# Two selective-scan layers on one Trainium2 core: sums of two groups take turns in the halves of one PSUM bank, their copies to y stand in four steps, and the short unit and the output stage share work differently

## The chip, the cores and the metric

The kernel runs on one core of a Trainium2 chip. A core has TensorE (PE; its weight loads are listed apart as PEld), VectorE (DVE), ScalarE (ACT) and GpSimd (POOL), which read and write 128 partitions of on-chip memory: SBUF, and PSUM, where PE leaves its results. SyncE (SP) issues the DMAs. The metric is the device time of one launch in microseconds; the median of three runs is given.

## The reference

The input x has 8 images of 64 x 64 positions with 96 channels. Two layers follow each other, each `x = x + conv_ref(groupnorm(x))`. Cut to what matters:

```python
# layer 0; layer 1 has the same frame
xp, z = split(x @ in_proj_w.T)                 # 192 channels each
xc = silu(depthwise_conv3x3(xp) + conv_b)
xs = cross_scan(xc)                            # 4 directions: by rows, by columns, both reversed
dts, Bs, Cs = split(x_proj(xs), [6, 16, 16])
delta = softplus(dt_projs(dts) + dt_bias)      # one per channel and position
def step(h, (u_t, d_t, B_t, C_t)):             # 16 states per channel, 4096 positions
    h = exp(d_t * A) * h + d_t * B_t * u_t
    return h, sum_states(h * C_t)
y = cross_merge(scan(step)) + u * D
out = (layernorm(y) * silu(z)) @ out_proj_w.T

# layer 1, in place of the recurrence
decay = exp(cumsum(dt * A))
h = decay * cumsum(dt * B * u / (decay + 1e-12))
y = sum_states(h * C) + u * D
```

In layer 1 `decay` falls to nothing after the first positions of a direction, and there h is nothing too. The kernel computes the first 160 positions of each direction at most, and fewer for the higher states.

## The kernel before

**Tiling.** Every image is done by itself. Its 4096 positions are cut into four pieces of T = 1024; the 192 channels into two halves of 96 and those into three groups of 32. One *set* is 32 channels x 4 states on the 128 partitions by 1024 positions. Four sets cover the 16 states of a group, twelve a *job* (a half of the channels in one piece of one direction), so an image has 32 jobs and 384 sets. One launch goes through a beginning and then, for each image, a layer-0 scan and an output stage. Layer 1 of the image before is not a stage by itself: its convolution and the preparation of its inputs lie beside the scan, its scan is a *short unit* of 6 sets (960 wide) at the end of the next image's sets, and its output stage is done together with that of the next image. The last image's layer 1 stands alone at the end, in `scan_last`.

**The scan's order.** `scan_rows` writes the order out by hand under `tc.manual_schedule()`, one set per step n. `at(i)` is set n + i. In one step every engine works at another set:

- SP: `fetch` and `replicate` (the broadcast loads of `dt_rep`, `dtu_rep`, `b_rep`, `c_rep`), four to five steps ahead.
- DVE: `advance_set(at(0))`: the product `set = drive * b` (L970; in three of four sets), then the scan itself (L983), in place in `set`.
- ACT: `keep_state` (L994, the last column), `fill(at(1))`: `decay = exp(rate * dt)` into one of two PSUM buffers (L936), `drive(at(2))`: a copy of `dtu` into a PSUM tile (L953) once in a group, `release(at(-4))`: four copies of 32 x 256 from the group's sums `acc` into y (L1065; the tile is named `map` in the profile) once in a group.
- POOL: `read_out(at(-1))`: `out = set * c` (L999), and `early(at(2))`: the product `dtu * b` of every fourth set (L960).
- PE: `collect(at(-3))`: for a group's first set four matmuls that put the skip term or the old y into the sums (L1026), and for each set four matmuls that add up the four states (`w_gather`, L1035). The sums stand in `acc`, one PSUM bank in a pool of one buffer.

After `collect` come the step's planned stages: `ps_dt` (L690) and the transposes `ps_sp` (L724) on PE, with ACT's steps on `arena` between them (L701, L702, L736 and others), which make dt and dt * u of the job after next; the projection `ps_proj` (L570); and the convolution of layer 1 (L1102, `ps_conv`, nine taps for each piece). Once in four steps (`late`, the step in which a new group's first set is collected) the planned stages stand ahead of `collect`.

A short set goes the same way with other parts: DVE makes the product (L970), one fused product with the gate (L973: `(cum + 1) * set`) and two scans (L978); ACT makes the gate, four tanh in place in `cum` (L947), the decay (L932) and a `drive` copy; PE has 16 matmuls per set (L1012, which is shown for two sets), and ACT scales the sums into `y_short` (L1055).

**The output stage.** `out_phase` goes through chunks of 512 positions, eight per layer and image. A table `order` gives each operation a lag in chunks, and every step issues each operation for another chunk: load; `first_sum` (POOL); `mean` (PE, L1529) and `centre` (DVE, L1606); `square` (ACT, L1572) and `second_sum` (POOL, L1599, in place in `sq`); `variance` (PE, L1550, one chunk into 32 rows of `ps_var`); `roots` (ACT) and a Newton step (DVE, L1522 to L1524) for four chunks at once, which leave 1/sqrt(var) in 32-row strips of `r`; `gates` (PE, the z part of the in-projection, L1543) and `silu` (ACT, L1589); `row` (PE, L1534: a matmul over all 128 rows of `r` with a picking matrix, which spreads one chunk's strip to 96 rows); `scale` (DVE, L1610); `affine` (ACT, L1577, twice, one for each half of the channels); `product` (POOL); `project` (PE, L1562, `ps_out`); `end` and `store`.

PSUM has eight banks of 128 x 512. The scan uses four for `decay`, two for `drive`, one for `acc` and one (`pmisc`) for all planned stages; the output stage two for `mean`, two for `ps_var`, two for z, one for `ps_r` and one for `ps_out`.

## Time and profile before

| what | value |
|---|---|
| median of three runs | 12128.35 us (12126.23 to 12153.42) |
| the profiled execution | 12140.8 us, span 12138.9 us, mean granted PE clock 0.765 |
| products with c on POOL (L999) | 3120 of 2364 ns, 7308.8 us |
| scans with a state on DVE (L983) | 2304 of 2344 ns, 5361.8 us |
| scans without a state on DVE (L983) | 768 of 2286 ns, 1743.0 us |
| decay on ACT (L936) | 3072 of 1115 ns, 3424.4 us |
| products with b on DVE (L970) | 2352 of 1198 ns, 2818.4 us |
| sums over states on PE (L1035) | 24576 of 518 ns, 2394.3 us |
| convolution on PE (L1102) | 4032 of 689 ns, 2201.6 us |
| copies of sums to y on ACT (L1065) | 3072 of 479 ns, 1471.7 us |

All of it is one execution on the chip, taken by the hardware profiler. An engine's busy time counts neither waits nor the issue of DMAs. PE's matmuls overlap in the pipeline, so that count times mean is more than the busy time, and the distance between the starts of two groups says what they cost PE. "L999" is line 999 of the kernel before; in the changed kernel the same operations stand a few lines lower. In the groups, "out<-in" are the program's names of tiles, followed by partitions x elements; after the second bar stand the idle time of the engine just before these instructions and what ended most of it. In the timeline a row gives the start, the length, the engine, the line, the operation with its tiles, and in brackets how long it waited and for what; x4 means that four such instructions are drawn together. In the windows a row begins with the stretch and its length and ends with the granted PE clock, the busy share of the DMA engines and GB/s.

By the trace's times the beginning ends at 127 us; the eight scans, each without its short unit, take 1275 to 1307 us; between two scans lie 99 us (after the first image) or 185 to 190 us with the short unit and the output stage of two layers. The end after the last scan takes from 11723 to 12139 us.

### The profile page before, as it was taken

The page shows a single profiled execution, that of the slowest core. Times are in us where ns is not written, and L with a number is a line of the kernel's source. Part 1 is how long each engine was busy: PE and PEld are TensorE (multiplying, and loading weights), DVE is VectorE, ACT ScalarE, POOL GpSimd, SP SyncE. Part 2 cuts the span into 40 slices and gives each one's busy share as a digit, 9 for nine tenths or more (in the row PEclk, how much of TensorE's full clock was granted, in tenths as well). Part 3 has the DMA queues.
Part 4 walks back from the last instruction along what each step waited for, and adds up shares of the span by engine and source line. Part 5 has one row for each costly group of instructions (what it writes and reads, how often), then busy time and mean ns, then how long its engine had stood idle before and what let it go on. Part 6 is the DMA issues. An engine that isn't in the chain of part 4 may idle for free. (4 is left out here: it accounts for less than half of the span.)

```text
span 12138.9 us, 147546 instructions
## 1 busy us (share of the span) xinstructions
PE 8813.3 (73%) x50950; PEld 4023.1 (33%) x50950; DVE 10895.6 (90%) x6783; ACT 9090.1 (75%) x14944; POOL 10525.2 (87%) x4751
## 2 busy tenths in 40 slices
PE   6765577777877777777777767877687776876567
PEld 2332233332333323333333323333333332333222
DVE  8999799997999979999799997999879998899985
ACT  6777677777777777777777777777777777777775
POOL 6999799996999969999699986999879997799983
PEclk7776677778777787777877788777787777877677
DMA  4444444444444444444444454444544445444441
GB/s 133 149 165 156 137 149 165 164 164 144 164 154 159 157 145 167 162 165 153 152 148 166 164 160 147 166 163 155 165 138 164 161 165 164 135 157 157 155 145 57
DMA packets 670708, 1862.43 MB, mean 153 GB/s; under 512 B 186728, under 2 KB 201486, under 8 KB 669949
## 3 DMA queue, kind: packets, MB, share of 16 engines
q1 hardware_dynamic: 662781, 1840.30, 45.8%
q10 hardware_dynamic: 7168, 12.59, 0.3%
q8 instruction: 405, 6.64, 0.2%
q14 instruction: 354, 2.90, 0.1%
HBM read 1539.34 MB, written 313.28 MB: 153 GB/s over the span
## 5 line engine op out<-in xcount | busy, mean ns | idle before, releaser
L999 POOL TENSOR_TENSOR out<-set,c_rep 128x1024 f32<-128x1024 f32 x3120 | 7308.8, 2364 | 820.1 <-PE acc L1035 350.2
L983 DVE TENSOR_TENSOR_SCAN set<-decay,state,set 128x1024 f32<-128x1024 f32 x2304 | 5361.8, 2344 | 360.0 <-ACT decay L936 118.6
L936 ACT ACTIVATE decay<-dt_rep,w_a 128x1024 f32<-128x1024 f32 x3072 | 3424.4, 1115 | 429.1 <-DVE set L983 427.2
L970 DVE TENSOR_TENSOR set<-drive,b_rep 128x1024 f32<-128x1024 f32 x2352 | 2818.4, 1198 | 35.2 <-DMA b_rep<-x_dblr 17.6
L1035 PE MATMUL acc<-out,w_gather 128*32 128x256 f32 x24576 | 2394.3, 518 | 8.5 <-POOL out L999 8.1
L1102 PE MATMUL ps_conv<-edged,taps 96*96 96x512 f32 (+1 forms) x4032 | 2201.6, 689 | 9.8 <-ACT arena L702 8.1
L960 POOL TENSOR_TENSOR set<-dtu_rep,b_rep 128x1024 f32<-128x1024 f32 x768 | 1856.8, 2418 | 96.9 <-DMA b_rep<-x_dblr 31.0
L983 DVE TENSOR_TENSOR_SCAN set<-decay,set 128x1024 f32<-128x1024 f32 x768 | 1743.0, 2286 | 147.7 <-ACT decay L936 53.1
L724 PE MATMUL ps_sp<-w_eye,arena 128*96 128x128 f32 x7680 | 1167.3, 317 | 707.0 <-ACT arena L736 672.9
L1026 PE MATMUL acc<-map,w_eye 96*32 96x256 f32 x4608 | 577.5, 584 | 1352.3 <-ACT map L1065 1085.4
L1065 ACT COPY map<-acc 32x256 f32<-32x256 f32 x3072 | 1471.7, 479 | 66.3 <-PE acc L1035 25.8
L724 PEld LDWEIGHTS ps_sp<-w_eye,arena 128*96 128x96 f32 x7680 | 1011.1, 148 | 1012.6 <-ACT arena L736 788.6
L1035 PEld LDWEIGHTS acc<-out,w_gather 128*32 128x32 f32 x24576 | 880.9, 140 | 1390.2 <-issue 1066.3
L994 ACT COPY state<-set 128x1 f32<-128x1 f32 x2304 | 433.1, 188 | 1061.2 <-DVE set L983 1053.3
L690 PE MATMUL ps_dt<-w_dtw,x_dbl 7*128 7x96 f32 x3840 | 803.1, 371 | 533.2 <-ACT arena L736 426.9
L1102 PEld LDWEIGHTS ps_conv<-edged,taps 96*96 96x96 f32 (+1 forms) x4032 | 701.9, 189 | 1275.5 <-issue 1188.6
L690 PEld LDWEIGHTS ps_dt<-w_dtw,x_dbl 7*128 7x128 f32 x3840 | 700.0, 269 | 778.5 <-ACT arena L736 499.9
L953 ACT COPY drive<-dtu_rep 128x1024 f32<-128x1024 f32 (+1 forms) x816 | 816.5, 1001 | 40.1 <-DMA dtu_rep<-dtu_far 19.2
L701 ACT ACTIVATE arena<-ps_dt 128x384 f32<-128x384 f32 x480 | 235.9, 492 | 647.1 <-PE ps_dt L690 631.0
L1026 PEld LDWEIGHTS acc<-map,w_eye 96*32 96x32 f32 x4608 | 104.0, 125 | 1676.3 <-ACT map L1065 1299.5
L600 POOL TENSOR_TENSOR arena<-arena,map 96x1024 f32<-96x1024 f32 x240 | 635.5, 2648 | 12.9 <-ACT arena L736 11.7
L570 PE MATMUL ps_proj<-map,w_wx 96*78 96x512 f32 x512 | 402.7, 923 | 9.9 <-ACT map L305 6.1
(204 smaller groups left out, 7718.6 us busy)
## 6 DMA issues: line engine op xcount, KB each, us to landing
dt_rep<-dt_far SPq DMA_DIRECT2D x768, 512.0 KB
dtu_rep<-dtu_far SPq DMA_DIRECT2D x768, 512.0 KB
b_rep<-x_dblr SPq DMA_DIRECT2D x256, 512.0 KB
c_rep<-x_dblr SPq DMA_DIRECT2D x256, 512.0 KB
b_rep<-x_dblc SPq DMA_DIRECT2D x256, 512.0 KB
c_rep<-x_dblc SPq DMA_DIRECT2D x256, 512.0 KB
dt_far<-arena SPq DMA_DIRECT2D x240, 384.0 KB
dtu_far<-arena SPq DMA_DIRECT2D x240, 384.0 KB
```

What stands on the lines that cost most here:

```text
L690: nc.tensor.matmul(job["ps"][:, j, :], unit["x_dbl"][: R + 1, at : at + P], w["dtw0"][:, k, h * C : (h + 1) * C], start=True, stop=True,)
L724: nc.tensor.matmul(job["ps"][:C, j * P : (j + 1) * P], job[name][:, s * BLOCKS + j, :], w["whole_eye"], is_transpose=True, start=i == 0, s ...
L936: nc.scalar.activation(s["decay"], s["group"]["dt"], AF.Exp, scale=rate)
L953: nc.scalar.copy(s["group"]["drive"], s["group"]["dtu"])
L960: nc.gpsimd.tensor_tensor(s["buf"], s["group"]["dtu"], b, ALU.mult)
L970: nc.vector.tensor_tensor(s["buf"], s["group"]["drive"], b, ALU.mult)
L983: nc.vector.tensor_tensor_scan(ordered(s["buf"], unit), ordered(s["decay"], unit), ordered(s["buf"], unit), 0.0 if unit["nth"] == 0 else s ...
L999: nc.gpsimd.tensor_tensor(s["out"], s["buf"], s["unit"]["c", s["i"]], ALU.mult)
L1026: nc.tensor.matmul(acc, lhs[:, GC * g : GC * (g + 1)], positions(old[:, h, :], unit["column"], unit["t0"] + at, n), start=True, stop=False ...
L1035: nc.tensor.matmul(acc, w["gather"], s["out"][:, at : at + n], start=False, stop=s["i"] == NS - 1, skip_group_check=True,)
L1065: nc.scalar.copy(yk, like(acc, unit["column"]))
L1102: nc.tensor.matmul(job["ps"][:C, :], taps[l][:k, h, tap, :], edged[:k, tap // 3 : tap // 3 + rows, tap % 3 : tap % 3 + WW], start=tap == 0 ...
```

## The change

There are three parts.

**The sums.** The bank `acc` is one tile for the whole scan, and its two halves of 256 columns are handed out in turn to the groups. `release` copies one of the four strips per step, at steps 4 to 7 after the group's last set; for the image's last whole group all four come at once. The `late` order is gone: `collect` always stands ahead of the planned stages. In `scan_last` two banks take turns, as the pool's two buffers did before.

**The short unit.** The product with b of a short set is made by POOL one step ahead, `gate` writes to a PSUM tile of the `drive` pool, and the copy `drive` is left out for short sets. The copies to `y_short` (now `release_short`) do not change.

**The output stage.** `row` is issued for two chunks at once, and each matmul reads only its 32-row strip of `r` and of the picking matrix; `ps_r` has two banks and `ps_var` one. `variance` is issued for four chunks at once; the sums of squares wait for it in `squares`, a tile with four buffers. The second half of `affine` goes from ACT to DVE. A chunk is loaded one step later, and `x_in` has six buffers.

```diff
@@ scan_rows
+                bank = pacc.tile([P, MM], F32, name="acc0")
+                accs = cycle([bank[:, : T // Q], bank[:, T // Q :]])
...
+                    last = n - 4 == whole - 1
...
-                    drive(at(2), False, pdrive)
-                    drive(at(1), True, pdrive)
-                    release(at(-4), y, beside)
-                    gate(at(1))
+                    drive(at(2), pdrive)
+                    release_short(at(-4), beside)
+                    for a in range(Q):
+                        release(at(-4 if last else -4 - a), a, y)
+                    gate(at(1), pdrive)
+                    early(at(1), True, work)
                     read_out(at(-1), work)
-                    early(at(2), work)
-                    late = (n + 1) % NS == 0
-                    if not late:
-                        collect(at(-3), xc, y, pacc)
+                    early(at(2), False, work)
+                    collect(at(-3), xc, y, accs)
                     for stage in plan.pop(n, []):
                         stage()
-                    if late:
-                        collect(at(-3), xc, y, pacc)
@@ by_gpsimd
-        return s["i"] == NS - 1
+        return s["i"] == NS - 1 or s["unit"]["short"]
@@ gate
+            s["gate"] = pdrive.tile([P, T], F32, name="drive")[:, :HT]
...
-                nc.scalar.activation(cum, cum, AF.Tanh, bias=half_log, scale=rate)
+                cum, out = blocks(s["group"]["cum"], i), blocks(s["gate"], i)
+                nc.scalar.activation(out, cum, AF.Tanh, bias=half_log, scale=rate)
@@ collect
-            group["acc"] = pacc.tile([P, MM], F32, name="acc0")
+            group["acc"] = next(accs)
@@ release(s, a, y): one strip a of a group
+        if not s or s["unit"]["short"] or s["i"] < NS - 1 or a in s.setdefault("gone", []):
             return
+        s["gone"].append(a)
-        for a in range(Q):
...
+        nc.scalar.copy(yk, like(acc, unit["column"]))
@@ out_phase
-            tc.tile_pool(name="pvar", bufs=2, space=PSUM) as pvar,
+            tc.tile_pool(name="pvar", bufs=1, space=PSUM) as pvar,
-            tc.tile_pool(name="prow", bufs=1, space=PSUM) as prow,
+            tc.tile_pool(name="prow", bufs=2, space=PSUM) as prow,
@@ row(c): nothing for odd c, else both chunks of the pair
+                for c in (c, c + 1):
+                    q = c % Q
+                    rows = slice(GC * q, GC * (q + 1))
...
+                        w["pick"][rows, q, :],
+                        groups[c // Q]["r"][rows, :],
@@ variance(c): nothing before the fourth chunk, then all four
+                for q in range(Q):
+                    nc.tensor.matmul(
+                        group["var"][GC * q : GC * (q + 1), :],
+                        w["avg"][:, :GC],
+                        held[c - Q + 1 + q].pop("squares"),
@@ affine
-                for h in range(NH):
...
+                nc.scalar.activation(
+                    first, first, AF.Identity, bias=shift[:, 0:1], scale=gain[:, 0:1]
+                )
+                nc.vector.tensor_scalar(
+                    second, second, gain[:, 1:2], shift[:, 1:2], ALU.mult, ALU.add
+                )
@@ second_sum
-                nc.gpsimd.tensor_tensor(sq[:, 0, :], sq[:, 0, :], sq[:, 1, :], ALU.add)
+                held[c]["squares"] = brief.tile([C, MM], F32, name="squares", bufs=Q)
+                nc.gpsimd.tensor_tensor(
+                    held[c]["squares"], sq[:, 0, :], sq[:, 1, :], ALU.add
+                )
@@ order
-                (load, 5), (mean, 1), (row, 8), (gates, 7), (variance, 3), (project, 10),
+                (load, 6), (mean, 1), (row, 8), (gates, 7), (variance, 3), (project, 10),
@@ loaded
-            x = xpool.tile([C, MM], F32, name="x_in", bufs=7)
+            x = xpool.tile([C, MM], F32, name="x_in", bufs=6)
```

More of the change, by code (lines that the diff above doesn't have):

```diff
@@ L2 @@
 from contextlib import ExitStack, contextmanager
+from itertools import cycle
 import concourse.bass as bass
@@ L446, in scan_rows @@
             total = len(sets)
+            whole = sum(not s["unit"]["short"] for s in sets)
             plan = plan(pmisc)
@@ L936, in fill, with gate, drive, early @@
         nc.scalar.activation(s["decay"], s["group"]["dt"], AF.Exp, scale=rate)
-    def gate(s):
+    def gate(s, pdrive):
         if s and s["unit"]["short"]:
+            s["gate"] = pdrive.tile([P, T], F32, name="drive")[:, :HT]
             for i in range(NS):
                 rate = w["a1_half"][:, column(s) + i :][:, :1]
-                cum = blocks(s["group"]["cum"], i)
-                nc.scalar.activation(cum, cum, AF.Tanh, bias=half_log, scale=rate)
-    def drive(s, short, pdrive):
-        if s and s["i"] == 0 and s["unit"]["short"] == short:
+                cum, out = blocks(s["group"]["cum"], i), blocks(s["gate"], i)
+                nc.scalar.activation(out, cum, AF.Tanh, bias=half_log, scale=rate)
+    def drive(s, pdrive):
+        if s and s["i"] == 0 and not s["unit"]["short"]:
             s["group"]["drive"] = pdrive.tile([P, T], F32, name="drive")[:, : s["unit"]["n"]]
             nc.scalar.copy(s["group"]["drive"], s["group"]["dtu"])
-    def early(s, work):
-        if s and by_gpsimd(s):
+    def early(s, short, work):
+        if s and by_gpsimd(s) and s["unit"]["short"] == short:
             s["buf"] = work.tile([P, T], F32, name="set", bufs=SETS)[:, : s["unit"]["n"]]
@@ L973, in advance_set @@
             nc.vector.scalar_tensor_tensor(
-                buf, s["group"]["cum"], 1.0, buf, ALU.add, ALU.mult
+                buf, s["gate"], 1.0, buf, ALU.add, ALU.mult
             )
@@ L999, in read_out, with collect @@
             nc.gpsimd.tensor_tensor(s["out"], s["buf"], s["unit"]["c", s["i"]], ALU.mult)
-    def collect(s, xc, y, pacc):
+    def collect(s, xc, y, accs):
         if not s:
@@ L1042, in collect, with release_short, release @@
             )
-    def release(s, y, beside):
-        if not s or s["i"] < NS - 1 and not s["unit"]["short"]:
+    def release_short(s, beside):
+        if not s or not s["unit"]["short"]:
             return
         unit, h, g = s["unit"], s["group"]["h"], s["group"]["g"]
-        if unit["short"]:
-            if h == g == 0:
-                ys_far[unit["b"]] = dram.tile([NH, P, NG * HEAD], F32, name="ys_far", bufs=2)
-            if g == 0:
-                unit["y"] = beside.tile([P, MM], F32, tag="conv_out", name="y_short")
-            part = unit["y"][:, g * HEAD : (g + 1) * HEAD]
-            nc.scalar.mul(part, s["group"]["acc"][:, :HEAD], 0.5)
-            if g == NG - 1:
-                nc.sync.dma_start(ys_far[unit["b"]][h], unit["y"][:, : NG * HEAD])
+        if h == g == 0:
+            ys_far[unit["b"]] = dram.tile([NH, P, NG * HEAD], F32, name="ys_far", bufs=2)
+        if g == 0:
+            unit["y"] = beside.tile([P, MM], F32, tag="conv_out", name="y_short")
+        part = unit["y"][:, g * HEAD : (g + 1) * HEAD]
+        nc.scalar.mul(part, s["group"]["acc"][:, :HEAD], 0.5)
+        if g == NG - 1:
+            nc.sync.dma_start(ys_far[unit["b"]][h], unit["y"][:, : NG * HEAD])
+    def release(s, a, y):
+        if not s or s["unit"]["short"] or s["i"] < NS - 1 or a in s.setdefault("gone", []):
             return
+        s["gone"].append(a)
+        unit, h, g = s["unit"], s["group"]["h"], s["group"]["g"]
         n = T // Q
-        for a in range(Q):
-            yk = positions(
-                y[GC * g : GC * (g + 1), h, :], unit["column"], unit["t0"] + a * n, n
-            )
-            acc = s["group"]["acc"][GC * a : GC * (a + 1), :n]
-            nc.scalar.copy(yk, like(acc, unit["column"]))
+        yk = positions(y[GC * g : GC * (g + 1), h, :], unit["column"], unit["t0"] + a * n, n)
+        acc = s["group"]["acc"][GC * a : GC * (a + 1), :n]
+        nc.scalar.copy(yk, like(acc, unit["column"]))
     def conv_beside(plan, pmisc, pool, edged, l, src, far, norm, starts, ends=None):
@@ L1271, in scan_last @@
                 tc.tile_pool(name="pdrive", bufs=1, space=PSUM) as pdrive,
-                tc.tile_pool(name="pacc", bufs=2, space=PSUM) as pacc,
+                tc.tile_pool(name="pacc", bufs=1, space=PSUM) as pacc,
                 tc.manual_schedule(),
             ):
+                accs = cycle([pacc.tile([P, MM], F32, name=f"acc{i}") for i in range(2)])
                 for n in range(-4, len(sets) + 4):
@@ L1281, in scan_last @@
                     fill(at(1), pslot)
-                    drive(at(1), True, pdrive)
-                    gate(at(1))
+                    gate(at(1), pdrive)
+                    early(at(1), True, work)
                     read_out(at(-1), work)
-                    collect(at(-2), xc, xc, pacc)
+                    collect(at(-2), xc, xc, accs)
                     add_sums(at(-3), xc)
@@ L1531, in row @@
             def row(c):
-                held[c]["r"] = prow.tile([P, MM], F32, name="ps_r")
-                lhs = w["pick"][:, c % Q, :]
-                nc.tensor.matmul(
-                    held[c]["r"][:C, :], lhs, groups[c // Q]["r"], start=True, stop=True
-                )
+                if c % 2:
+                    return
+                for c in (c, c + 1):
+                    q = c % Q
+                    rows = slice(GC * q, GC * (q + 1))
+                    held[c]["r"] = prow.tile([P, MM], F32, name="ps_r")
+                    nc.tensor.matmul(
+                        held[c]["r"][:C, :],
+                        w["pick"][rows, q, :],
+                        groups[c // Q]["r"][rows, :],
+                        start=True,
+                        stop=True,
+                    )
             def gates(c):
@@ L1546, in variance @@
             def variance(c):
-                group, q = groups[c // Q], c % Q
-                if q == 0:
-                    group["var"] = pvar.tile([P, MM], F32, name="ps_var")
-                nc.tensor.matmul(
-                    group["var"][GC * q : GC * (q + 1), :],
-                    w["avg"][:, :GC],
-                    held[c].pop("sq")[:, 0, :],
-                    start=True,
-                    stop=True,
-                    skip_group_check=True,
-                )
+                if c % Q < Q - 1:
+                    return
+                group = groups[c // Q]
+                group["var"] = pvar.tile([P, MM], F32, name="ps_var")
+                for q in range(Q):
+                    nc.tensor.matmul(
+                        group["var"][GC * q : GC * (q + 1), :],
+                        w["avg"][:, :GC],
+                        held[c - Q + 1 + q].pop("squares"),
+                        start=True,
+                        stop=True,
+                        skip_group_check=True,
+                    )
             def project(c):
@@ L1575, in affine @@
                 l = stream(c)[0]
-                for h in range(NH):
-                    nc.scalar.activation(
-                        part(c)[:, h, :],
-                        part(c)[:, h, :],
-                        AF.Identity,
-                        bias=w[f"lb{l}"][:, h : h + 1],
-                        scale=w[f"lg{l}"][:, h : h + 1],
-                    )
+                gain, shift = w[f"lg{l}"], w[f"lb{l}"]
+                first, second = part(c)[:, 0, :], part(c)[:, 1, :]
+                nc.scalar.activation(
[3 more added lines that the diff above has]
+                    second, second, gain[:, 1:2], shift[:, 1:2], ALU.mult, ALU.add
+                )
             def silu(c):
@@ L1597, in second_sum @@
             def second_sum(c):
-                sq = held[c]["sq"]
-                nc.gpsimd.tensor_tensor(sq[:, 0, :], sq[:, 0, :], sq[:, 1, :], ALU.add)
+                sq = held[c].pop("sq")
+                held[c]["squares"] = brief.tile([C, MM], F32, name="squares", bufs=Q)
+                nc.gpsimd.tensor_tensor(
+                    held[c]["squares"], sq[:, 0, :], sq[:, 1, :], ALU.add
+                )
             def product(c):
```

## The prediction

> **What bounds the kernel now.** I read the share of busy time first, then the same by stage, then who waited for whom, then single moments. The stages below are one image: its scan (2992 to 4299 us), the short unit before it (2805 to 2845) and the output stage (2845 to 2992, with its dense middle from 2899 to 2943).

> ```profile
> PE 8813.3 (73%) x50950; PEld 4023.1 (33%) x50950; DVE 10895.6 (90%) x6783; ACT 9090.1 (75%) x14944; POOL 10525.2 (87%) x4751
> ```
> ```profile
> 2805.00:2845.00 40.00, 14.85 (x186) 10.78 (x187) 31.43 (x26) 32.53 (x64) 16.71 (x9) 0.66 0.68 228
> 2845.00:2992.00 147.00, 129.04 (x313) 41.05 (x310) 85.94 (x100) 108.05 (x158) 87.47 (x50) 0.91 0.47 140
> 2992.00:4299.00 1307.00, 982.62 (x5916) 457.83 (x5916) 1231.36 (x710) 992.66 (x1655) 1205.64 (x531) 0.76 0.47 157
> ```
> ```profile
> 2899.00:2943.00 44.00, 43.06 (x101) 13.99 (x100) 30.55 (x41) 41.26 (x56) 28.33 (x17) 1.00 0.19 57
> ```

> Columns after the length: busy PE, PEld, DVE, ACT, POOL, then PE's granted clock. The scan is DVE's: 1231 of 1307 us, POOL close behind. So at most 76 us per image can be won there, and only what DVE waits for counts. The dense middle of the output stage is PE's (43.1 of 44) with ACT at its heels (41.3).

> ```profile
> PE acc L1026 <- ACT map L1065: 1300.8, 266, 11.8
> ACT arena L701 <- PE ps_dt L690: 631.0, 374, 15.1
> POOL out L999 <- PE acc L1035: 350.2, 306, 3.8
> DVE set L983 <- ACT decay L936: 171.8, 144, 11.1
> DVE set L983 <- POOL set L960: 94.0, 105, 3.5
> ```
> ```profile
> 3019.08 1.49 ACT L1065 COPY map<-acc 32x256 f32<-32x256 f32 x4
> 3020.62 1.08 PE L1026 MATMUL acc<-map,skip 96*32 96x256 f32 x8 [5.71 <-ACT map L1065]
> 3022.72 2.38 POOL L999 TENSOR_TENSOR out<-set,c_rep 128x1024 f32<-128x1024 f32 x1 [1.34 <-PE acc L1035]
> ```

> The chain to see: four copies on ACT, PE's next group behind the last of them, POOL's `out` behind PE, and in the end DVE behind POOL's `set` (94.0) or ACT's `decay` (171.8).

> **Part 1, the sums (scan).** The instruction order of the two built programs, with what each waits for, shows more than the diff: the halves are one tile to the dependency tracking. In the changed program every collect on PE waits for the copy of its own step, and every copy waits for the collect of the step before. No copy runs beside a collect; the gain is that PE waits for one copy, not four, every fourth step.

> Removed: 4 copies take 1.49 us together, one 0.48, so the first collect of a group starts 1.0 us earlier, and it no longer stands behind the step's planned matmuls (L690 takes 803.1/480 = 1.7 us for four). Moved: in the old `late` steps `ps_dt`, `ps_sp` and convolution taps now queue behind a collect (2394.3/3072 = 0.78 us, with L1026 about 1.3). The 1.0 us pays for most of that. Added: a copy ahead of ACT's planned stages in three more steps. Behind a waiting copy stand ACT's stages of that step, the state copy and the decay two sets ahead, for which DVE waits.

> When does PE make a copy late? A convolution tap costs 2201.6/(224 x 9) = 1.09 us. Three steps of three taps are 3 x (0.78 + 3.28) = 12.2 us of PE against 9.4 to 10.5 us of DVE (a set is 3.57, one in four 2.27). PE ends 2 to 3 us behind, and a copy waits only for the collect one step earlier, 2.3 to 3.6 us before it: cover about equal to lag. So in most steps the new wait costs nothing; without the cover it costs what PE lags.

> Gain: the 350.2 us of POOL behind PE mostly goes; it costs the end only through the 94.0 us of DVE, of which I take two thirds, 63. Of the 171.8 us behind `decay`, much lies at an image's start and in its last two jobs; I take 17. Sum **-80 us**, between -266 (both waits gone) and plus the lockstep rival below.

> **Part 2, the short unit** (48 sets, seven images and the end).

> ```profile
> 2825.30 2.21 POOL L999 TENSOR_TENSOR out<-set,c_rep 128x960 f32<-128x960 f32 x1 [3.42 <-DVE set L978]
> 2826.27 2.25 DVE L973 SCALAR_TENSOR_TENSOR set<-cum_rep,set 128x960 f32<-128x960 f32 x1
> 2846.24 1.73 PE L1012 MATMUL acc<-out,w_gather 128*32 128x160 f32 x32 [0.48 <-ACT y_short L1055]
> 2848.00 0.30 ACT L1055 ACTIVATE y_short<-acc 128x160 f32<-128x160 f32 x1 [1.91 <-PE acc L1012]
> ```

> DVE loses the product L970 (1.14 us), ACT the `drive` copy (0.94), POOL gains one product (2.2). The gate moves to PSUM: L973 takes 1.16 us with POOL still, up to 2.27 with POOL at work, and L970, which has a PSUM input, 1.13 to 1.21 either way; so I price it at 1.2. Per set DVE falls from 5.63 to 1.2 + 2.2 = 3.4, POOL rises to 4.4, ACT is at 1.95 + 2.02 + 0.3 = 4.3: 5.63 becomes about 4.5, at most 7 us per unit. [...]

> Two things stand behind it. The DMA engines are 0.92 to 0.98 busy from 2810 to 2830 us with these loads. And the six collects go back and forth with L1055, 1.73 + 0.30 + 0.2 = 2.2 us each after the last whole group's copies (2828 us), 13.4 us whatever DVE does. I take -2.5 in each of seven images and -5 at the end: **-22 us**, between 0 and -55.

> **Part 3, the output stage.**

> ```profile
> L1577 ACT ACTIVATE map<-map,w_lb,w_lg 96x512 f32<-96x512 f32 x144 | 108.6, 802 | 4.0 <-DVE map L1610 3.9
> L1550 PE MATMUL ps_var<-sq,w_avg 96*32 96x512 f32 x256 | 152.0, 679 | 1.8 <-POOL sq L1599 1.6
> L1534 PE MATMUL ps_r<-r,w_pick 128*96 128x512 f32 x256 | 149.5, 668 | 30.3 <-DVE y L1610 27.4 <-DVE map L1610 2.8
> 3025.91 0.64 PE L1035 MATMUL acc<-out,w_gather 128*32 128x256 f32 x8
> ```

> At full clock a chunk costs PE, by the distance of starts, 0.95 (mean) + 0.86 (row) + 1.81 (z) + 0.97 (variance) + 1.80 (out) = 6.4 us, and chunks follow each other at 6.4 us in the timeline: PE's pace. The last line is the evidence for four variances in one go: four matmuls into four 32-row strips take 0.64 us, where one of twice the length (L1550) takes 1.04. Four variances should take about 1.25 us, not 3.9: -0.66 per chunk. Two rows of 32 inputs in different strips: nothing in this trace is packed so; between -0.43 (side by side) and 0; I take -0.26, as L1035 is the nearest row. [...]

> ACT loses one of two L1577 (1.51 to 0.80), DVE gains a scaling (L1266: 0.74 us for 1024 wide, so 0.4). Load one step later: the chunk is needed a step, 4 to 6 us, after issue rather than two; no PE wait on `x_in` stands in the waits, so nothing, else a few us per image. New wait: `squares` has four buffers, so once in four chunks POOL's second sum waits for the packed variances, up to 4 us with its product and PE's projection queued behind; POOL has 28 of 44 us of work there, which covers most of it.

> So 6.4 becomes about 5.7 in some nine steps (-6), 0.3 less in eight later ones (-2.5), 1.5 at the start: -10 per full stage. Six of these, -5 for the first image's half, -8 for the last image's, -9 for the final eight chunks, whose chain of waits is nearly all PE: **-82 us**, between -15 and -150.

> **Sum.** 12140.8 (span 12138.9, 1.9 around it) - 80 - 22 - 82 = 11957. That execution is 12 us above the median of 12128.35, inside the runs' spread; I say 11950.

> **Rivals.**
> *A, the scan gives nothing* (chance 0.22): DVE's wait moves from POOL to ACT, as ACT's total is unchanged. For it: ACT waits 631 us for `ps_dt`, which now stands behind a collect. Against: that collect starts earlier. Parts 2 and 3 alone: 12140.8 - 104 = 12037.
> *B, lockstep, slower* (0.14): a copy each step, held by PE, holds `decay`. Place: the three convolution steps and the `ps_dt` pair of each of 256 jobs. At 1 us of DVE per job it is +256 - 104 = +152, 12290; it decides from 104/256 = 0.4 us per job. For it: ACT's load in the first four steps of a job leaves DVE little cover. Against: the cover worked out above, and 1053.3 us that ACT spends waiting for DVE.
> *C, packing gives little* (0.12): POOL's new wait for `squares`, or ACT, takes PE's place: part 3 is -15, in all 12024.
> *Forecast* (0.52): around 11950, its own range 11850 to 12040.

> Measurement tells 0.3% (36 us) from no change. The forecast is on the faster side but for 0.02; A and C are faster but for 0.03 each; B is slower but for 0.02. With some room for what I have not seen: faster 0.77, same 0.08, slower 0.15. The range reaches to A and C and to a mild B, 12130, and down to most of the scan's waits gone with full packing, 11820.

> **What would show it.** Right: PE's wait for `map` copies cut to well under half, POOL's for `acc` below 120 us, DVE's for `set` on POOL below 40; four variances within 1.4 us; chunks 5.7 apart; short sets 4.5 apart. Wrong: a large wait of ACT's copies on `acc` with DVE's wait for `decay` above 250 (B), a POOL wait on `ps_var` (C), or PE's clock in the output stage falling from 0.91 because it now pauses.

## The result and the profile after: 2.25% slower

The changed kernel takes 12408.67 us (median of 4 runs, 12385.75 to 12422.67) against 12128.26 us before: a ratio of 1.0225, 95% interval 1.0208 to 1.0242. The profiled execution has a span of 12408.9 us, 270 more than before, at a mean granted PE clock of 0.742 (0.765).

By stage, from the starts of the first and last full set of every image, the loss lies in the scans alone:

| stretch | before, us | after, us | change |
|---|---|---|---|
| eight scans | 10352.0 | 10691.4 | +339.4 |
| seven stretches between scans | 1241.7 | 1207.3 | -34.4 |
| after the last scan | 418.2 | 382.6 | -35.6 |

The share of busy time (the page), and the windows of one image's short unit, output stage and scan:

```profile
PE 9085.6 (73%) x50950; PEld 3745.1 (30%) x50950; DVE 10891.7 (88%) x6863; ACT 8990.9 (72%) x14768; POOL 10632.7 (86%) x4799
```
```profile
2907.00:2946.00 39.00, 18.69 (x213) 11.11 (x212) 21.11 (x20) 28.13 (x59) 28.32 (x13) 0.74 0.71 235
2946.00:3087.00 141.00, 119.62 (x295) 37.16 (x293) 95.08 (x115) 96.70 (x141) 86.08 (x50) 0.83 0.47 137
3087.00:4437.00 1350.00, 1015.08 (x5905) 424.10 (x5906) 1231.18 (x711) 995.05 (x1654) 1207.80 (x532) 0.75 0.46 153
```

DVE does the same work as before in the scan (1231 us) and needs 1350 us for it in place of 1307. It waits more, and the waits say for whom:

```profile
PE acc L1039 <- ACT map L1071: 1772.2, 1312, 7.1
ACT map L1071 <- PE acc L1039: 837.3, 603, 4.8
PE acc L1030 <- ACT map L1071: 549.2, 200, 5.0
POOL out L1003 <- PE acc L1039: 450.4, 353, 4.0
DVE set L987 <- ACT decay L939: 341.1, 222, 11.0
DVE set L987 <- POOL set L964: 96.0, 71, 3.7
```

The first line is new, and the second was 25.8 us before: PE's sums wait for the copies, and the copies for the sums. DVE's wait for `decay` has doubled (171.8 before), POOL's for the sums has grown (350.2). Two other waits of DVE for ACT have grown too. Before, then after:

```profile
DVE arena L862 <- ACT arena L844: 73.5, 16, 22.7
DVE conv_out L1115 <- ACT conv_out L1112: 8.3, 11, 1.4
```
```profile
DVE arena L865 <- ACT arena L847: 138.9, 16, 21.0
DVE conv_out L1121 <- ACT conv_out L1118: 102.9, 38, 7.7
```

The first is the running sum that prepares the inputs of the short unit, the second DVE's part of the convolution, which comes after ACT's tanh. Single moments show the chain. The job is one of the scan above; the moments are from 3600 us on.

```profile
3600.87 5.44 PE L1108 MATMUL ps_conv<-edged,taps 96*96 96x512 f32 x6
3608.24 0.59 ACT L1071 COPY map<-acc 32x256 f32<-32x256 f32 x1 [2.75 <-PE acc L1039]
3611.95 0.60 ACT L1071 COPY map<-acc 32x256 f32<-32x256 f32 x1 [1.16 <-PE acc L1039]
3616.87 1.28 ACT L720 ACT_TABLE_LOAD   x1
3618.16 0.84 ACT L721 ACTIVATE arena<-arena 128x768 f32<-128x768 f32 x1
3618.99 1.11 ACT L939 ACTIVATE decay<-dt_rep,w_a 128x1024 f32<-128x1024 f32 x1
3620.14 2.35 DVE L987 TENSOR_TENSOR_SCAN set<-decay,state,set 128x1024 f32<-128x1024 f32 x1 [1.83 <-ACT decay L939]
3620.67 1.05 PE L1030 MATMUL acc<-map,w_eye 96*32 96x256 f32 x8 [3.80 <-ACT map L1071]
3622.74 2.37 POOL L1003 TENSOR_TENSOR out<-set,c_rep 128x1024 f32<-128x1024 f32 x1 [2.28 <-PE acc L1039]
```

Three taps hold PE for 5.44 us at a granted clock of 0.50 (at 1.00 two take 1.96 us, at 3611.82), so the next sums are late; the copies behind them cost ACT 2.75 and 1.16 us; ACT has no slack left when its densest steps come (`drive`, a table load, the logarithm), `decay` is late and DVE waits 1.83 us; the copy is late as well, and PE and then POOL wait for it in turn.

DVE's idle time in the eight scans went from 545 to 877 us, by 333, which is nearly all of the loss. Sorted by the set of a job that it stands ahead of (the first set is set zero), it grew at two places above all. Ahead of set eight 61 us became 293: the wait for `decay` went from 8.0 to 179.6, that for `arena` from 29.1 to 99.1, and the distance from the start of set seven to that of set eight from 3.71 to 4.62 us in the mean of all jobs. Ahead of set nine 36 us became 129, of which 100.5 behind the tanh. Ahead of set five DVE waits 48 us less than before, ahead of set seven 35 more. ACT's copies waited 257 and 224 us while DVE was at sets four and five, and another 228 at set eight.

### The profile page after: what moved, and what is told of

Read it like the earlier page. It is cut to its first block, busy times and chain, and to the rows that moved or that the text cites. A ratio compares the mean times of both kernels' runs of the same rounds, so it can differ in the third digit from the quotient of the medians.

```text
span 12408.9 us, 149448 instructions
## 1 busy us (share of the span) xinstructions
PE 9085.6 (73%) x50950; PEld 3745.1 (30%) x50950; DVE 10891.7 (88%) x6863; ACT 8990.9 (72%) x14768; POOL 10632.7 (86%) x4799
## 5 line engine op out<-in xcount | busy, mean ns | idle before, releaser
L1039 PE MATMUL acc<-out,w_gather 128*32 128x256 f32 x24576 | 2550.4, 494 | 2011.6 <-ACT map L1071 1772.2
L1108 PE MATMUL ps_conv<-edged,taps 96*96 96x512 f32 (+1 forms) x4032 | 2538.0, 772 | 8.1 <-ACT arena L705 8.1
L964 POOL TENSOR_TENSOR set<-dtu_rep,b_rep 128x1024 f32<-128x1024 f32 (+1 forms) x816 | 1964.7, 2408 | 247.0 <-DMA b_rep<-x_dblr 56.9
L1071 ACT COPY map<-acc 32x256 f32<-32x256 f32 x3072 | 1471.4, 479 | 902.3 <-PE acc L1039 837.3
L1039 PEld LDWEIGHTS acc<-out,w_gather 128*32 128x32 f32 x24576 | 697.2, 126 | 3761.8 <-issue 2435.8
L727 PE MATMUL ps_sp<-w_eye,arena 128*96 128x128 f32 x7680 | 1268.7, 336 | 65.7 <-ACT arena L739 64.5
L727 PEld LDWEIGHTS ps_sp<-w_eye,arena 128*96 128x96 f32 x7680 | 1099.4, 158 | 393.8 <-issue 170.3
L957 ACT COPY drive<-dtu_rep 128x1024 f32<-128x1024 f32 x768 | 768.6, 1001 | 65.1 <-DMA dtu_rep<-dtu_far 43.9
L693 PE MATMUL ps_dt<-w_dtw,x_dbl 7*128 7x96 f32 x3840 | 573.8, 291 | 172.2 <-ACT arena L705 64.1
L693 PEld LDWEIGHTS ps_dt<-w_dtw,x_dbl 7*128 7x128 f32 x3840 | 491.2, 196 | 390.4 <-ACT arena L705 179.2
L739 ACT COPY arena<-ps_sp 96x512 f32<-96x512 f32 x480 | 280.2, 584 | 176.9 <-PE ps_sp L727 165.8
```

What stands on the lines that cost most here:

```text
L693: nc.tensor.matmul(job["ps"][:, j, :], unit["x_dbl"][: R + 1, at : at + P], w["dtw0"][:, k, h * C : (h + 1) * C], start=True, stop=True,)
L727: nc.tensor.matmul(job["ps"][:C, j * P : (j + 1) * P], job[name][:, s * BLOCKS + j, :], w["whole_eye"], is_transpose=True, start=i == 0, s ...
L957: nc.scalar.copy(s["group"]["drive"], s["group"]["dtu"])
L964: nc.gpsimd.tensor_tensor(s["buf"], s["group"]["dtu"], b, ALU.mult)
L1039: nc.tensor.matmul(acc, w["gather"], s["out"][:, at : at + n], start=False, stop=s["i"] == NS - 1, skip_group_check=True,)
L1071: nc.scalar.copy(yk, like(acc, unit["column"]))
```

## The experiments

Every ratio is to the kernel before, run on the same chip in turn. The first two runs take the change apart.

**The sums alone** (part 1 on the kernel before).

> Part 1 of the change alone on the kernel before; short unit and output stage as before. Between the two profiles the eight scans became 336 us longer together and all stretches between them and after them about 70 us shorter. If the sums alone make the scans longer (all of theories 1 to 3 below), this is 12128 + 336 = about 12465 us. Theory 1, lockstep: on the one tile every collect waits for the copy of its own step and every copy for the collect of the step before. Theory 2, order: the planned matmuls stand behind the collect in the one step of four where they stood ahead of it. Theory 3, spread: ACT has a copy ahead of its planned stages in every step, whether the copy waits or not. If instead the other parts disturb the scans (a lower PE clock carried over from the output stage, other buffers), this is well below, 12300 or less.

12441.19 us, ratio 1.0265 (1.0240 to 1.0289); scans 10646 us. Part 1 by itself lengthens the scans by 294 of the 339 us; what the other 45 are is open.

**The rest alone** (parts 2 and 3, sums as before).

> Parts 2 and 3 alone: short unit and output stage as changed, sums, their copies and the order of the scan as before. From the stretches outside the scans: 12128 - 70 = about 12058 us by theories 1 to 3, with scans as long as before. If the other parts disturb the scans: 12150 or more.

12090.51 us, ratio 0.9960 (0.9943 to 0.9976): a small gain, half of it between the scans and half after the last. The scans have nearly their old length (10369 us against 10352).

**The old order kept** (one edit to the changed kernel):

```diff
-                    collect(at(-3), xc, y, accs)
+                    late = (n + 1) % NS == 0
+                    if not late:
+                        collect(at(-3), xc, y, accs)
                     for stage in plan.pop(n, []):
                         stage()
+                    if late:
+                        collect(at(-3), xc, y, accs)
```

> The changed kernel with one edit: in the one step of four in which a new group's first set is collected the planned stages stand ahead of the collect again, as before; one tile for both halves, copies in four steps. Theory 2 (order): the scans come back, about 12060 us. Theory 1 (lockstep): the mutual waits stay, and in those steps the collect is later still, so no gain: 12380 to 12550 us. Theory 3 (spread): 12400 us.

12542.31 us, ratio 1.0339 (1.0322 to 1.0356). Theory 2 falls: with the old order it is slower still, and the copies' wait for the sums rises from 837.3 to 1413.7 us, as lockstep has it.

**Two banks.** The simplest test would be two tiles of 256 columns in place of one tile with two halves. But as built each of them takes a whole bank, and PSUM then has none left for `pmisc`, so there is no time for that version, and a bank had to be made free.

```diff
# both, cut: drive in one bank, the gate back in SBUF
-            s["gate"] = pdrive.tile([P, T], F32, name="drive")[:, :HT]
+            s["gate"] = s["group"]["cum"]
...
-            s["group"]["drive"] = pdrive.tile([P, T], F32, name="drive")[:, : s["unit"]["n"]]
-            nc.scalar.copy(s["group"]["drive"], s["group"]["dtu"])
+            s["group"]["drive"] = pdrive.tile([P, MM], F32, name="drive")
+            for i in range(T // MM):
+                nc.scalar.copy(s["group"]["drive"], s["group"]["dtu"][:, i * MM :][:, :MM])
...
# the second only: a bank for each of two groups
-                bank = pacc.tile([P, MM], F32, name="acc0")
-                accs = cycle([bank[:, : T // Q], bank[:, T // Q :]])
+                accs = cycle([pacc.tile([P, MM], F32, name=f"acc{i}")[:, : T // Q] for i in range(2)])
```

> Control for the next run: the changed kernel with the tile drive folded to one PSUM bank, which frees a bank that stays empty here. ACT writes both halves of dtu over each other in two copies, and DVE reads the bank twice, so the products with b use the second half's dtu in both halves; the short unit's gate stands in SBUF, in place in cum. Sums as changed: one tile, two halves. All theories: close to the changed kernel, 12380 to 12480 us, with ACT waiting about 840 us in its copies for the sums.

> As the control (the same part of the computation left out), but the two groups' sums stand in two banks, two tiles, with the freed bank; order and number of instructions as in the changed kernel. Theory 1, lockstep: collects and copies of different groups no longer wait for each other; ACT's wait in its copies falls below 200 us, PE's for the copies below 700, and the time falls by the whole loss of the scans or more, 340 to 450 us under the control, about 12020. Theory 3, the spread of the copies itself: within 60 us of the control.

12471.5 us (ratio 1.0280, 1.0250 to 1.0310) for the control, 12063.06 (0.9954, 0.9931 to 0.9976) with two banks: 408 us apart, by one edit that moves no instruction. The waits of the control, then of the two banks:

```profile
ACT map L1074 <- PE acc L1042: 894.2, 605, 4.7
DVE set L990 <- ACT decay L939: 354.3, 271, 10.3
POOL out L1006 <- PE acc L1042: 509.1, 382, 4.2
```
```profile
ACT map L1073 <- PE acc L1041: 10.0, 16, 4.2
ACT map L1073 <- PE acc L1032: 19.8, 97, 1.2
PE acc L1032 <- ACT map L1073: 1276.6, 235, 12.0
DVE set L989 <- ACT decay L938: 149.9, 97, 11.1
POOL out L1005 <- PE acc L1041: 74.0, 92, 2.5
```

The copies' waits for sums have dropped from 894.2 us to 29.8. PE still waits 1276.6 us for copies, where below 700 was expected, but the scans are not longer for it. Theory 3 falls (the copies are as spread as in the control) and lockstep stands. But look at the scans: 10335 us, 17 less than before the change. With POOL's wait for the sums down from 350 to 74 us, DVE still gained next to nothing (in the scan ACT has one more short copy per group here, as in the control).

**Few taps.** What makes the sums late?

```diff
-            for tap in range(first, first + n):
+            for tap in set(range(first, first + n)) & {0, 8}:
```

> The kernel before with two of the nine taps of each convolution piece beside the scan (the first and the last; seven are left out). DVE sets the scan, so little moves: 12030 to 12130 us by all theories.

> The changed kernel with the same two of nine taps. What makes the copies late? If it is the taps, which stand on PE between one collect and the next (about 1.1 us each at mean clock, three in a step), most of the loss goes: at most 100 us over the run before with few taps, ACT's wait in its copies below 300 us. If the collects are late for another reason (behind POOL, behind the copies themselves), the loss stays, 230 us or more over it.

12031.99 us before (ratio 0.9918, 0.9889 to 0.9947) and 12062.35 changed (0.9947, 0.9927 to 0.9966): 30 us apart in place of 280. Both differences contain what the other parts gained outside the scans; in the scans alone it is 79 us (10268 to 10347) in place of 339. So most of the loss needs the taps. In the changed kernel with few taps:

```profile
PE acc L1039 <- ACT map L1071: 2530.3, 1770, 5.3
ACT map L1071 <- PE acc L1039: 303.9, 460, 2.1
DVE set L987 <- ACT decay L939: 126.8, 75, 11.1
```

PE waits more than ever, and DVE waits less for `decay` than in the kernel before; the copies wait 0.66 us a time in place of 1.39 (303.9 us in all, where below 300 was expected). Most of the 79 us that are left stand ahead of set eight, behind `arena` (L847): 28.7 us with few taps before, 98.5 here. The granted clock is 0.645, lower than in the slow kernel (0.742), and the scans still take 344 us less than there (10347 us against 10691): a low mean PE clock alone did not make them long. With all the taps it is a part of the chain: the first three taps of a piece took PE 4.94 us in the mean in the changed kernel, 3.95 before and 3.89 with two banks, and the clock granted while DVE was at set three of a job was 0.53, 0.67 and 0.75. How much of the loss the slower taps make is not separated.

**Copies together** (the changed kernel, `release(at(-4), a, y)` for every strip), and **together with the old order** (the diff of the old order on top).

> The changed kernel with one edit: all four copies of a group stand in one step again, four steps after its last set; the halves take turns and no planned stage stands ahead of a collect. Collects and copies now meet once in a group, not in every step. Theory 1 (lockstep in every step behind the taps): the scans come back to within 60 us of before, 12050 to 12150 us, with ACT's wait in its copies below 150 us. If the lost order of the planned stages, or the halves as such, cost the time: 12300 us or more.

> The changed kernel with its four copies in one step and with the planned stages ahead of the collect in the one step of four, as before: of part 1 only the turn of the two halves is left. If that order is what the run with the copies in one step had lost (12171 against 12090 us for the other two parts alone), it comes back here: 12070 to 12110 us, and DVE's wait for set eight of a job is gone. If the halves themselves cost it: 12150 us or more.

12171.48 us (ratio 1.0027, 1.0016 to 1.0038) and 12074.99 (0.9965, 0.9951 to 0.9979). The first lies above its range: something is left. It is the order, as the second shows, which is back at the level of the rest alone. The line that says why is in the waits of the first, and one of its moments shows how:

```profile
ACT conv_out L1118 <- PE ps_conv L1108: 226.8, 82, 8.1
```
```profile
9656.99 0.64 PE L1030 MATMUL acc<-map,w_eye 96*32 96x256 f32 x8 [3.59 <-ACT map L1071]
9658.15 3.73 PE L1108 MATMUL ps_conv<-edged,taps 96*96 96x512 f32 x4
9671.26 0.59 ACT L1118 ACTIVATE conv_out<-ps_conv 96x512 f32<-96x512 f32 x1 [6.26 <-PE ps_conv L1108]
9675.12 2.29 DVE L987 TENSOR_TENSOR_SCAN set<-decay,set 128x1024 f32<-128x1024 f32 x1 [5.50 <-ACT decay L939]
```

In the rest alone the wait for the taps is 37 us. Here taps stand behind a collect that waits for four copies. PE pauses for 3.59 us, its next taps take 3.73 us for two (1.96 in the changed kernel at a granted clock of 1.00), and ACT stands still in the convolution's tanh, with `decay` queued behind it. So part 1, taken apart in this order, is: halves 0 (0.9965 against 0.9960), the order dropped +0.6%, the copies spread +2.0%. The order is worth something while the copies meet the sums once in a group; once they meet in every step it is harmful, as it makes the sums later for the next copy.

**The output stage.** Why did it gain so little? Two guesses.

```diff
-                (load, 6), (mean, 1), (row, 8), (gates, 7), (variance, 3), (project, 10),
+                (load, 6), (mean, 1), (variance, 3), (row, 8), (gates, 7), (project, 10),
```

> Short unit and output stage as changed, sums as before (12090 us in the run of those two parts alone), with one edit: on PE the four packed variances stand ahead of the rows and the gates of their step, so that squares comes free sooner. If POOL's wait for ps_var (73 us in all in that run, some 11 in the middle of each of six full stages) is what takes the packing's gain: that wait below 25 us, the middle of a stage 3 to 5 us shorter, 12050 to 12070 us. If the lower granted PE clock (0.82 to 0.89 there against 0.95 before) takes it: 12080 to 12100 us.

12110.32 us, ratio 0.9979 (0.9969 to 0.9988), against 0.9960 for the rest alone: if anything slower. POOL's wait for `ps_var` fell from 73 to 35 us, but the middle of a full stage (first to last mean) went from some 90.0 to 91.8 us, as ACT's silu waits longer for the gates that were pushed back. That wait was not the limit, and the time is above both ranges.

> Both edits in one: the changed kernel with the four copies in one step and the variances ahead of rows and gates. If the two do not touch each other: the time of the first of these runs less what the second gains, 12020 to 12130 us. Of interest is whether it lies below the kernel before by more than 0.3%.

12215.18 us, ratio 1.0054 (1.0036 to 1.0072), above its range and slower than with the copies together alone; the two edits add up (0.3% and 0.2%).

```diff
+            def fill_gap():
+                ps = po.tile([P, MM], F32, name="ps_out")
+                for _ in range(6):
+                    nc.tensor.matmul(ps[:C, :], w["avg"], held[2]["x"], start=True, stop=True)
+            if len(streams) > 1:
+                plan.setdefault(9, []).insert(0, fill_gap)
```

> Short unit and output stage as changed, sums as before (12090 us in the run of those parts alone), and six added matmuls of 96 x 512 into the free ps_out bank, once in each of the seven stages with two layers, on PE ahead of the planned matmul that waits 5.96 us for DVE there; their result is used by nobody. In that run PE's granted clock is 0.50 over the 12 us after that wait (0.90 and more later), and the kernel before, which waits 2.21 us there, is back at full rate 6 us later. If the packing's gain is lost because PE now pauses there and is slowed for it: the clock behind the gap 0.85 or more, the middle of a stage 4 to 8 us shorter, 12035 to 12065 us though PE does more. If the pause is not the cause: 12085 to 12110 us.

PE in the rest alone, at the pause and behind it (timeline; two gates, L1554, take 1.96 us at 2930.73, at a granted clock of 1.00):

```profile
2894.13 2.02 PE L622 MATMUL ps_dt<-x_dbl,w_dtw 7*96 7x512 f32 x2 [5.96 <-DVE y L1623]
2899.98 3.73 PE L1554 MATMUL ps_z<-x_in,zw 96*96 96x512 f32 x4
2910.73 2.29 PE L1554 MATMUL ps_z<-x_in,zw 96*96 96x512 f32 x4
```

The same place with the pause filled, and a later one:

```profile
2881.71 5.31 PE L1497 MATMUL ps_out<-x_in,w_avg 96*96 96x512 f32 x12
2887.95 1.09 PE L622 MATMUL ps_dt<-x_dbl,w_dtw 7*96 7x512 f32 x2 [0.93 <-DVE y L1631]
2891.03 1.96 PE L1562 MATMUL ps_z<-x_in,zw 96*96 96x512 f32 x4
2942.75 3.70 PE L1584 MATMUL ps_out<-map,w_out 96*96 96x512 f32 x4 [1.90 <-DVE x_in L1747]
```

With the pause filled PE goes on at a granted clock of 1.00 (2882 to 2906; 0.50 from 2894 to 2906 in the rest alone), and the middle of a stage is 86 us in place of 90. That this pause went with the slower PE is shown; what filling it is worth is not: 12071.8 us, ratio 0.9957 (0.9940 to 0.9973), no better than the rest alone. After a pause of 1.90 us at 2941 PE runs at half rate for some 20 us (granted clock 0.53 from 2942 to 2954 and 0.62 from 2954 to 2966), and from the last mean to the next scan it takes 55.3 us or more in four stages of six where the rest alone takes 48.5 to 49.0. In the one of these six without that pause it takes 49.2.

## Why the prediction was wrong

**The failing step** is in part 1: "cover about equal to lag. So in most steps the new wait costs nothing". The sum behind it took three taps at 3.28 us, by a mean over both clock rates, and asked for one copy at a time. In the changed kernel the first three taps of a piece took 4.94 us (3.95 before), at a granted clock of 0.53 over set three of a job (0.67 before). (DVE's side is 3 x 3.57 = 10.7 us at most, not 10.5.) And lags add up from step to step, because in lockstep a late copy makes the next collect late, and ACT cannot make up the 3.9 us of the two waits in the timeline above before its densest steps. The price appears not where the wait is (sets four and five) but at sets eight and nine, three steps on and more. Rival B had the mechanism, the place (the convolution steps) and the sign that would show it, DVE's wait for `decay` above 250 us (it is 341.1). It was mis-sized, 1.0 us per job where the scans show 339.4/256 = 1.33, and it was given a chance of 0.14. The new dependency was known from the built programs; averages of cover and lag that came out equal were no ground to price it at nothing.

**The gain of part 1** (-80 us) was not there either. With two banks POOL's wait for the sums went to 74 us, and the scans gained 17. Of the 94 us for which DVE waits for POOL's `set`, 81 are left in that run, so POOL is late mostly for other reasons than its waits for the sums. Its own load (87% busy before) may be one; but with few taps in the kernel before the 94 us fell to 36.8, so PE's taps have a part in it. The cause stays open.

**Part 2.** The pace of 4.5 us came only in the unit at the end (4.53 us, 5.88 before). In the seven others the gated products start 5.6 us apart in the mean (5.4 before); in the unit shown here the distances are 7.95, 5.18, 4.59, 6.39 and 4.48. The sum went by the work of the busiest engine and left out the wait of DVE for ACT's gate. Before, then after:

```profile
DVE set L973 <- ACT cum_rep L947: 36.4, 26, 4.6
```
```profile
DVE set L977 <- ACT drive L951: 98.4, 44, 5.2
```

In the rest alone the seven are at 5.1 us, so a part of this comes with the sums. The stretch from the last full set to the first mean gained 1.2 us per unit (45.2 to 44.0), where 2.5 was forecast: the chain named there, six collects in turn with the scaling to `y_short`, begins only after the last whole group's copies:

```profile
4453.07 1.16 DVE L977 SCALAR_TENSOR_TENSOR set<-drive,set 128x960 f32<-128x960 f32 x1 [1.21 <-ACT drive L951]
4457.67 1.16 DVE L977 SCALAR_TENSOR_TENSOR set<-drive,set 128x960 f32<-128x960 f32 x1 [1.20 <-ACT drive L951]
4459.45 2.39 ACT L1071 COPY map<-acc 32x256 f32<-32x256 f32 x4
4461.99 3.07 PE L1016 MATMUL acc<-out,w_gather 128*32 128x160 f32 x32 [5.30 <-ACT map L1071]
4477.18 1.73 PE L1016 MATMUL acc<-out,w_gather 128*32 128x160 f32 x32 [0.48 <-ACT y_short L1058]
```

**Part 3.** The packing's price was right; in the rest alone four variances take 1.06 us and two rows 1.10 (1.03 to the next start, which saves 0.34 per chunk, between the 0.26 taken and the 0.43 side by side):

```profile
2929.70 1.10 PE L1541 MATMUL ps_r<-r,w_pick 32*96 32x512 f32 x4
2932.61 1.06 PE L1564 MATMUL ps_var<-squares,w_avg 96*32 96x512 f32 x8
```

At a granted clock of 1.00 (2918 to 2942) chunks follow at 5.6 us there (means at 2924.40, 2928.74 and 2935.52), 5.7 forecast. But the middle of a stage is no shorter than before, because the work that PE lost became pauses (7 us of idle per 90 us before, 14 after), and PE's clock in the stage fell from 0.91 to 0.83: the last of the signs named as wrong. In all the stretches outside the scans gained 70 us, where 104 was forecast.

**The new total:** 12140.8 + 339 - 70 = 12410, which is the profiled execution.

Why are the halves ordered at all? The built programs order collects and copies by the whole tile, which is one bank, and the two-bank run shows what that costs (12063.06 us against 12471.5). An order by single strips was not tried, and no run here leaves a collect and a copy in one bank unordered.

## What to carry to other kernels

Two halves of one PSUM bank were no double buffer here: sums and copies still waited for each other (1772.2 and 837.3 us). That cost nothing while they met once in a group and the planned stages kept their old order, and 2% or more once the copies were spread over the steps; with two banks the copies waited 29.8 us and the scans took 10335 us. Before a wait is priced by cover, follow what stands behind the waiting instruction to its engine's densest steps: here lost slack was paid there and not where the wait was. Of the versions run that compute the whole, three lie below the kernel before by 0.3 to 0.4% (the rest alone, the same with the pause filled, and halves with the copies together and the old order); none can be told from the others.
